# Last attention of a two-layer kernel: values weighed in two phases of two query tiles instead of three phases

## The chip, the cores and the metric

The kernel runs on one core of a Trainium2 chip. The metric is the device time of one execution in microseconds (us); the median of three runs is 1755.78 us (1751.4 to 1757.81).

## The reference

Four sequences of 512 tokens with 256 features pass through two layers. Each layer is an attention and a feed-forward part, each behind a layer norm and added to the residual stream:

1. a linear attention with decay in blocks, and a feed-forward part with Walsh-Hadamard transforms;
2. a softmax attention without a mask (16 heads of 16 features), and then a block that holds a causal attention and a mixture of experts.

The change lies in that last block. Its attention has 32 query heads of 64 features over 8 key and value heads and rotary tables; the mixture takes 4 of 16 experts for each token:

```python
q, k = _rope(q, k)                                   # 32 query heads, 8 key/value heads of 64
k = jnp.repeat(k, g, axis=2)
v = jnp.repeat(v, g, axis=2)
scores = jnp.einsum('bqhd,bkhd->bhqk', q, k) / np.float32(np.sqrt(HEAD_DIM))
scores = jnp.where(causal[None, None], scores, jnp.float32(-1e+30))
attn = jax.nn.softmax(scores, -1)
o = jnp.einsum('bhqk,bkhd->bqhd', attn, v).reshape(B, S, NHEADS * HEAD_DIM)
x = x + o @ wo
h = _rms(x, ff_ln_w)
logits = h @ wg
topv, topi = jax.lax.top_k(logits, TOP_K)
gate = jax.nn.softmax(topv, -1)
```

## The kernel before, in words

The stages follow one another: first layer, attention of 16 heads, last attention, mixture of experts. The order of the instructions in the last two is written out by hand, so each engine runs its queue in the order of the program text. The last attention takes from about 694 us to 1435 us of the span.

**Units and steps.** A unit `u` (16 of them) is one sequence and one pair of key/value heads: 8 query heads, four query tiles `t` of 128 tokens. A unit has five steps `f`, and the main loop counts them as `n = 5u + f`; `v = u - 1` is the unit before. In every step `fill(n)` puts scores into four PSUM banks (`sc`, one for each of four row groups `s`), `least(n)` on VectorE masks them into `masked` and takes the smallest of each row (the scores are negated), `exps(n, s)` on ScalarE makes exponentials in place and their sums, and one step later `turn_blocks(n)` on VectorE transposes blocks of 32 x 32 into `pT`. `FILLS` says which query tiles a step holds: before, tile 3 takes steps 0 and 1 (one half of the heads `jj` each), tiles 0 and 2 share steps 2 and 3, tile 1 has step 4. `masked` has one buffer for each `s`, so `least(n)` follows `turn_blocks(n - 1)`; the four `sc` banks have one set, so `fill(n + 1)` follows `least(n)`.

**Weighing the values.** `weigh(u, phase, ...)` multiplies `pT` by the values. It works on tiles of 32 rows by 64 columns of the array: for each chunk `c` of 32 keys, each row group `a` of four and each half `g`, one product whose moving operand is 4 heads x 32 queries = 128 columns, or 256 columns where two query tiles of a phase still need that chunk. A product stands as two matmul instructions in the profile (fp32). Its sums stay in four banks (`heaps`). Before there are three phases: `"3"` (tile 3 alone, 16 chunks, at the end of step 4), `"02"` (tiles 0 and 2, 12 chunks, end of step 0 of the next unit) and `"1"` (tile 1, 8 chunks, end of step 1). `weighed` on VectorE multiplies the heap by the widened inverse sums into `oT`, at the start of the next step, ahead of that step's `turn_blocks`.

**Inverse sums and output.** `invert` takes reciprocals, `widen` on ScalarE spreads them over 64 columns, `inverses` transposes them on TensorE and copies them to `rsb`; `out_proj` multiplies `oT` by the output weights, and ScalarE and GpSimd add the result to `zs`.

**Banks.** Eight PSUM banks: four for `sc`, and four (`unit`) that all else shares in turn: heaps, `pq` of the inverses, `py` of the output, `pr` of the rotary projections (`q_lo`, `q_hi`, `keys_lo`, `keys_hi`), `pv` of the values, and those of the routing. A heap of four banks thus waits until the last four users have been copied out. These copies are held back by `drain` and placed among the exponentials by the string of the step: a `.` is one held copy, a `w` one `widen`, a digit one `exps`. What is left over goes after the exponentials.

**Extra pieces.** Layer norms of the next sequence and the routing of the one before (`route(b)`, ending in `choose` and 16 scatters into `xs`) are queues of small pieces, of which `extras(plain, banked, scatters)` takes a few per step. `plan_tiles(0)` then makes the tables of the first expert tiles, and `read_plan(0)` reads them. `plan_tiles(1)` and the routing of the last sequence are pieces among the expert tiles.

**Transfers.** `spread(u, i)` loads a quarter of the values of unit `u` into `vsr` by four transfers on the SP queue; `fetch_q`, `twice` and the writes to `vd` use the same queue.

Of the kernel before, what the change touches and what calls it, by code (L numbers as in the profile page):

```python
# [16 lines left out]
P = 128  # L17
B = 4
S = 512
# [70 lines left out]
def kernel(  # L90
# [1207 lines left out]
    with ExitStack() as a2:  # L1298
# [20 lines left out]
        def spread(u, i):  # L1319

            if i == 0:
                vsrs[u] = ap2.tile([P, 16, P], F32, tag="vsr", bufs=2, name="vsr")
            part = slice(4 * i, 4 * i + 4)
            for a in range(4):
                nc.sync.dma_start(
                    out=vsrs[u][rows(a), part, :], in_=vds[u // 2][u % 2, :, part, :]
                )
# [3 lines left out]
            ((3, 0, 0),),  # L1331
            ((3, 1, 0),),
            ((0, 0, 0), (2, 0, P)),
            ((0, 1, 0), (2, 1, P)),
            ((1, 0, 0), (1, 1, 2 * P)),
        )

        PARTS = {"3": ((3, 0),), "02": ((0, 0), (2, P)), "1": ((1, 0),)}
        PHASE_OF = ("3", "3", "02", "02", "1")
# [47 lines left out]
        def turn_blocks(n):  # L1387

            u, f = divmod(n, 5)
            phase = PHASE_OF[f]  # L1390
            if (u, phase) not in turned:
                turned[u, phase] = [
                    ap2.tile([P, 4, S], F32, tag=f"pT{g}", bufs=2, name="pT4")
                    for g in range(2)
                ]
            for s, p in enumerate(probs.pop(n)):
                dst = turned[u, phase][s % 2]
                if f < 4:
                    nc.vector.transpose(dst[:, 2 * (f % 2) + s // 2, :], p)  # L1399
                else:  # L1400
                    for jj in range(2):
                        nc.vector.transpose(
                            dst[:, 2 * jj + s // 2, : 2 * P],
                            p[:, 2 * P * jj : 2 * P * (jj + 1)],
                        )


        def weigh(u, phase, lo, hi):
            if lo == 0:
                heaps[u, phase] = [  # L1410
                    unit("po4") for _ in range(4)
                ]
            for c in range(lo, hi):
                for a in range(4):
                    on = [
                        i for i, (t, _) in enumerate(PARTS[phase]) if 4 * t + a >= c
                    ]
                    if not on:
                        continue
                    first, last = on[0], on[-1] + 1  # L1420
                    for g in range(2):
                        src = turned[u, phase][g][rows(a), :, :]
                        if len(on) == 2:
                            src = src.rearrange("p j (x n) -> p x j n", n=P)
                            src = src[:, 0:2, :, 32 * c : 32 * c + 32]
                        else:
                            at = PARTS[phase][first][1] + 32 * c
                            src = src[:, :, at : at + 32]
                        nc.tensor.matmul(  # L1429
                            heaps[u, phase][a][  # L1430
                                64 * g : 64 * g + 64, first * P : last * P
                            ],
                            lhsT=vsrs[u][rows(a), c, 64 * g : 64 * g + 64],
                            rhs=src, start=(c == 0), stop=(4 * PARTS[phase][first][0] + a == c),
                            skip_group_check=True,
                        )

        def invert(n):

            u, f = divmod(n, 5)  # L1440
            if f in (1, 3, 4):
                for t, _ in PARTS[PHASE_OF[f]]:
                    nc.vector.reciprocal(lots[u, "rs"][:, t, :], lots[u, "sm"][:, t, :])
# [8 lines left out]
        def inverses(u, t):  # L1452

            pq = unit("pq4")
            wide = wides.pop((u, t)).rearrange("p (j g) n -> p j (g n)", g=2)
            for j in range(4):
                nc.tensor.transpose(pq[:, tok(j)], wide[:, j, :], ident)  # L1457
            rsb[u, t] = ap2.tile([P, S], F32, tag="rsb", bufs=2, name="rsb")
            to = rsb[u, t]
            drain(lambda: nc.scalar.copy(to, pq))  # L1460

        def weighed(u, phase):
            heap = heaps.pop((u, phase))
            del turned[u, phase]
            for i, (t, _) in enumerate(PARTS[phase]):
                inv = rsb.pop((u, t)).rearrange("p (j n) -> p j n", j=4)
                oTs[u, t] = ap2.tile([P, 4, P], F32, tag="oT4", bufs=3, name="oT4")
                for a in range(4):
                    nc.vector.tensor_tensor(  # L1469
                        oTs[u, t][:, :, 32 * a : 32 * a + 32],  # L1470
                        heap[a][:, i * P : (i + 1) * P].rearrange("p (j n) -> p j n", j=4),
                        inv[:, :, 32 * a : 32 * a + 32], ALU.mult,
                    )

        def out_proj(u, t):
            py = unit("py4")
            oT = oTs.pop((u, t))
            for j in range(4):
                nc.tensor.matmul(  # L1479
                    py[:, :D], lhsT=oT[:, j, :], rhs=wo4[:, 4 * (u % 4) + j, :],  # L1480
                    start=(j == 0), stop=(j == 3),
                )
            z = zs[u // 4][:, t, :]

            def leave():
                y = ap2.tile([P, D], F32, tag="y4", bufs=2, name="y4")
                nc.scalar.copy(y, py[:, :D])  # L1487
                nc.gpsimd.tensor_tensor(z, z, y, ALU.add)  # L1488

            drain(leave)  # L1490
# [225 lines left out]
        def plan_tiles(phase):  # L1716

            lo, hi = PHASES[phase]
            pos = C("iota")

# [8 lines left out]
            wide = [P, NEXP, NEXP]  # L1729
# [9 lines left out]
            nc.vector.tensor_tensor(tiles, tiles, taken, ALU.subtract)  # L1739
            nc.vector.tensor_tensor(  # L1740
# [3 lines left out]
            nc.vector.tensor_reduce(first, cube, AX.X, ALU.add)  # L1744
            mine, past = small("mine"), small("past")
# [6 lines left out]
            if phase == 0:  # L1752
# [20 lines left out]
                nc.vector.tensor_tensor(place, place, ahead, ALU.add)  # L1773
            info = rp.tile([P, 5, NEXP], F32, tag="info", name="info")
# [83 lines left out]
        for n in range(5 * NU + 4):  # L1858
# [12 lines left out]
            if u % 4 == 0 and f == 4 and 0 < u < 4 * B:  # L1871
                later.extend(route(u // 4 - 1))
                if u // 4 == B - 1:
                    later.append((False, lambda: plan_tiles(0)))
                    later.append(("pause", lambda: None))
                    later.append((False, lambda: read_plan(0)))
# [7 lines left out]
            if on and u % 2 == 0:  # L1884
                if u > 0 and f < 4:
                    spread(u, f)
                if f == 4:
                    spread(u + 1, 0)
            elif on and f < 3:
                spread(u, f + 1)  # L1890
# [4 lines left out]
            if f < 3 and v >= 0:  # L1895
                weighed(v, ("3", "02", "1")[f])
            if 0 < n <= 5 * NU:
                turn_blocks(n - 1)
                invert(n - 1)
            if v >= 0:  # L1900
                if f == 0:
                    inverses(v, 0)
                    inverses(v, 2)
                if f == 1:
                    inverses(v, 1)
                    out_proj(v, 3)
                if f == 2:
                    out_proj(v, 0)
                    out_proj(v, 2)
                if f == 3:  # L1910
                    out_proj(v, 1)
            if on:
# [6 lines left out]
                if f == 4:  # L1919
                    inverses(u, 3)  # L1920
                    q_hi(2 * u + 3)
# [5 lines left out]
                if f == 1 and u % 2 == 1:  # L1927
                    extras(0, 1)


                wide = {0: [(v, 1)] if v >= 0 else [], 3: [(u, 3)], 4: [(u, 0), (u, 2)]}
                for i in ("..w0123", "..0.1.23", ".0.12.3", "w.0.12.3", ".ww.0123")[f]:
                    if i == "w":
                        if wide[f]:
                            widen(*wide[f].pop(0))
                    elif i == ".":
                        drain_one()
                    else:
                        exps(n, int(i))
            elif f == 0 and v >= 0:  # L1940
                widen(v, 1)
# [7 lines left out]
            if f == 0 and v >= 0:  # L1949
                weigh(v, "02", 0, 12)  # L1950
            if f == 1 and v >= 0:
                weigh(v, "1", 0, 8)
                del vsrs[v]
            if f == 4 and on:
                weigh(u, "3", 0, 16)
# [9 lines left out]
        pieces += [lambda: plan_tiles(1)] + 5 * [lambda: None] + [lambda: read_plan(1)]  # L1965
# [332 lines left out]
```

## Time and profile before

| What | Value |
|---|---|
| median of three runs | 1755.78 us |
| profiled execution: time, span | 1759.42 us, 1757.6 us |
| TensorE clock granted, mean | 0.962 |
| TensorE busy | 1626.2 us (93%) |
| VectorE, ScalarE, GpSimd busy | 1011.9, 826.7, 895.9 us |
| matmul instructions of `weigh` (L1429) | 8064 |
| `fill` of unit 0 starts; weights of the first expert are issued | 693.8 us; 1435.5 us |
| a unit, mean over units 1 to 12 | 44.9 us |

In the profile a group of instructions stands as line, engine, operation, output<-inputs, shapes and count, then its busy time and the mean of one instruction, then the idle time of the engine before it with what ended that idle time. In a timeline the first two columns are start and length in us, and square brackets hold the idle time before. Lengths of matmuls are modelled: they overlap one another, so that a start is worth more than an end. L numbers are lines of the kernel.

### The profile page before, as it was taken

Reading aid. Unit: us, or ns where it says so; the run is one execution under the profiler, and the core shown is the slowest. Engines: PE = TensorE matmul, PEld = TensorE weight load, DVE = VectorE, ACT = ScalarE, POOL = GpSimd, SP = SyncE. Lnnn points to the kernel's source line nnn. Section 1 sums busy time; section 2 is a strip of 40 time slices with the busy share of each in tenths; the row PEclk is TensorE's granted clock in tenths of the full one; section 3 lists DMA queues with packets and bytes.
Section 4 is the critical chain, followed back from the end, with each engine's and each line's share of the span. In section 5 each row is a group of like instructions: output and inputs, shape, how many; then the busy total and the mean of one; then the engine's idle time right before and its main releaser. Section 6 shows DMA issues by size and latency. Waiting matters only on the chain.

```text
span 1757.6 us, 42136 instructions
## 1 busy us (share of the span) xinstructions
PE 1626.2 (93%) x16100; PEld 952.7 (54%) x16100; DVE 1011.9 (58%) x3097; ACT 826.7 (47%) x2170; POOL 895.9 (51%) x914
## 2 busy tenths in 40 slices
PE   7999999999999999899999999999999858899993
PEld 4665554553333334566666666666666635455551
DVE  4547336556665613767776686768766934433333
ACT  4431122126555575566666666665656514233331
POOL 4224133216555496655466647795577145744442
PEclk9999999999998899999999999999999969899997
DMA  9992000010000011222222222222132047655556
GB/s 358 370 371 87 0 1 0 1 55 1 1 1 1 1 31 48 92 56 56 54 59 56 56 56 56 84 75 59 43 86 70 3 164 225 147 87 87 87 87 167
DMA packets 106935, 146.60 MB, mean 83 GB/s; under 512 B 11632, under 2 KB 86128, under 8 KB 106352
## 3 DMA queue, kind: packets, MB, share of 16 engines
q1 hardware_dynamic: 91856, 123.54, 22.9%
q0 software_dynamic: 14448, 19.80, 6.5%
q8 instruction: 131, 2.15, 0.5%
q14 instruction: 68, 0.56, 0.1%
q10 hardware_dynamic: 432, 0.55, 0.1%
HBM read 67.17 MB, written 68.29 MB: 77 GB/s over the span
## 4 chain that ended last, share of the span: by engine, by line
PE 75%; DVE 7%; ACT 6%; POOL 5%; issue 4%; DMA 2%; SPq 0%; DVEq 0%; ACTq 0%; POOLq 0%
PE ph L1991 8%; PE po L1429 8%; PE sc L1352 7%; PE pgu L225 6%; PE py L1479 6%; PE py L234 6%; PE pr L225 5%; PE sT L1164 5%; PE sc L329 4%; PE pyx L1991 4%; PE oT L1177 3%; PE pq L225 2%; ACT masked L1382 2%; PE pv L234 2%; PE pq L1457 1%
## 5 line engine op out<-in xcount | busy, mean ns | idle before, releaser
L1382 ACT ACTIVATE masked<-masked,mx 128x256 f32<-128x256 f32 (+3 forms) x512 | 281.1, 553 | 13.6 <-DVE mx L1370 13.6
L1370 DVE CUSTOM_DVE_ANT_0 masked<-sc,cst 128x256 f32<-128x256 f32 (+3 forms) x512 | 213.9, 480 | 18.5 <-PE sc L1352 18.5
L1429 PE MATMUL po<-pT,vsr 32*64 32x128 f32 (+1 forms) x8064 | 186.6, 286 | 31.0 <-issue 16.0
L1399 DVE STREAM_TRANSPOSE pT<-masked 128x512 f32<-128x512 f32 x256 | 168.1, 690 | 57.3 <-ACT masked L1382 56.9
L335 DVE TENSOR_REDUCE top<-sc 128x1 f32<-128x512 f32 x256 | 158.7, 681 | 62.0 <-PE sc L329 62.0
L1429 PEld LDWEIGHTS po<-pT,vsr 32*64 32x64 f32 x8064 | 153.3, 131 | 75.1 <-issue 26.8
L2073 POOL DMA_INDIRECT acc<-yx,goes x79 | 123.3, 1561 | 138.3 <-ACT yx L2072 98.7
L1352 PE MATMUL sc<-kr,qr 32*128 32x128 f32 (+3 forms) x2048 | 180.8, 467 | 7.0 <-DVE mx L1370 4.4
L1991 PE MATMUL ph<-wall,hTx 128*128 x316 | 162.6, 638 | 10.5 <-DVE hTx L2029 10.1
L1170 ACT ACTIVATE pT<-sT 128x512 f32<-128x512 f32 x256 | 131.7, 602 | 59.2 <-PE sT L1164 59.2
L1488 POOL TENSOR_TENSOR z<-z,y 128x256 f32<-128x256 f32 x64 | 47.5, 743 | 182.5 <-ACT y L1487 182.4
L1469 DVE TENSOR_TENSOR oT<-po,rsb 128x128 f32<-128x128 f32 x256 | 61.5, 286 | 119.1 <-PE po L1429 112.3
L2053 DVE TENSOR_TENSOR ax<-ph,gx 128x256 f32<-128x256 f32 x79 | 33.5, 424 | 163.8 <-ACT gx L2051 163.7
L1352 PEld LDWEIGHTS sc<-kr,qr 32*128 32x128 f32 x2048 | 95.0, 194 | 58.7 <-issue 32.2
L1012 POOL TENSOR_TENSOR part<-raw,rtab 128x512 f32<-128x512 f32 x80 | 102.7, 1284 | 46.3 <-ACT raw L1003 42.9
L1479 PE MATMUL py<-wo,oT 128*128 128x256 f32 x512 | 123.6, 390 | 1.6 <-DVE oT L1469 1.6
L225 PE MATMUL pr<-hT,wq 128*128 128x512 f32 x256 | 122.8, 603 | 0.0
L1164 PE MATMUL sT<-qr,km 32*128 32x512 f32 x512 | 110.5, 650 | 6.4 <-DVE top L335 3.5
L225 PE MATMUL pgu<-xnT,wug 128*128 128x512 f32 x256 | 114.5, 598 | 1.5 <-DVE xnT L190 1.5
L1479 PEld LDWEIGHTS py<-wo,oT 128*128 128x128 f32 x512 | 94.9, 193 | 30.0 <-DVE pT L1399 7.6
L1006 POOL TENSOR_TENSOR qr<-raw,rtab 128x512 f32<-128x512 f32 x64 | 80.9, 1286 | 33.1 <-ACT raw L1003 33.1
L1382 ACT ACTIVATION_READ_ACCUMULATOR masked<-masked,mx 128x1 f32 x512 | 97.6, 191 | 0.0
(307 smaller groups left out, 2823.6 us busy)
## 6 DMA issues: line engine op xcount, KB each, us to landing
xs<-zero SPq DMA_DIRECT2D x16, 2304.0 KB
vsr<-vd SPq DMA_DIRECT2D x256, 64.0 KB
wall<-in_w_exp_dram SPq DMA_DIRECT2D x16, 768.0 KB
xin<-xs SPq DMA_DIRECT2D x79, 144.0 KB
wq<-in_w_q_dram SPq DMA_DIRECT2D x33, 256.0 KB
kr<-krq SPq DMA_DIRECT2D x32, 256.0 KB
acc<-zero SPq DMA_DIRECT2D x2, 2176.0 KB
vd<-vs SPq DMA_DIRECT2D x64, 64.0 KB
```

Source lines behind the costliest of these rows:

```text
L225: nc.tensor.matmul(dst, lhsT=w[:, c, cols], rhs=srcT[:, c, tok], start=(c == 0), stop=(c == n - 1),)
L234: nc.tensor.matmul(dst, lhsT=srcT[:, i, tok], rhs=w[:, c, cols], start=(i == 0), stop=(i == len(chunks) - 1),)
L335: nc.vector.tensor_reduce(top[:, at : at + 1], sc, AX.X, ALU.max)
L1164: nc.tensor.matmul(us[g], lhsT=km[rows(g), tok(c)], rhs=qr[rows(g), :], start=True, stop=True,)
L1170: nc.scalar.activation(pT[:, g, :], us[g], AF.Exp)
L1352: nc.tensor.matmul(scs[s][:, at : at + w], lhsT=qrs[2 * u + jj][rows(s), ab, tok(t)], rhs=krs[u][rows(s), ab, :w], start=(ab == 0), stop=( ...
L1370: nc.vector.tensor_tensor_reduce(masked[:, part], sc[:, part], C("cmask")[:, S - (t + 1) * P :], 1.0, 3e38, ALU.add, ALU.min, mx[:, t, i : ...
L1382: nc.scalar.activation(part, part, AF.Exp, bias=lots[u, "mx"][:, t, i : i + 1], scale=-1.0, accum_out=lots[u, "sm"][:, t, i : i + 1],)
L1399: nc.vector.transpose(dst[:, 2 * (f % 2) + s // 2, :], p)
L1429: nc.tensor.matmul(heaps[u, phase][a][64 * g : 64 * g + 64, first * P : last * P], lhsT=vsrs[u][rows(a), c, 64 * g : 64 * g + 64], rhs=src ...
L1479: nc.tensor.matmul(py[:, :D], lhsT=oT[:, j, :], rhs=wo4[:, 4 * (u % 4) + j, :], start=(j == 0), stop=(j == 3),)
L1991: ins = nc.tensor.matmul(out, lhsT=lhsT, rhs=wall[:, bass.ds(w_at[i] + at, n)], **kw)
```

## The change

- `FILLS` is reordered: tiles 0 and 2 in steps 0 and 1, tile 1 in step 2, tile 3 in steps 3 and 4.
- `weigh` has two phases `h`: tiles 0 and 1 (8 chunks) at the end of step 4, tiles 2 and 3 (16 chunks) at the end of the next step 0. The products become 168 for a unit instead of 252; those of 256 columns become 104 instead of 20, those of 128 columns 64 instead of 232.
- `pT` is kept by phase, with one buffer instead of two; `vsr` has one buffer instead of two; its loads go to steps 1 to 4.
- `weighed` writes its result over the inverse sums in `rsb`: 8 instructions of 256 columns instead of 16 of 128.
- Inverses, widenings and output projections move between steps: one output projection in each of steps 0 to 3; tile 3's inverse is taken, widened and transposed in step 0 of the next unit.
- `plan_tiles` is a generator in four pieces; in the last three units `extras(0, 1)` is also called in the middle of steps 0 and 4, ahead of the exponentials.

```diff
-vsrs[u] = ap2.tile([P, 16, P], F32, tag="vsr", bufs=2, name="vsr")
+vsrs[u] = ap2.tile([P, 16, P], F32, tag="vsr", bufs=1, name="vsr")
 FILLS = (
-    ((3, 0, 0),),
-    ((3, 1, 0),),
     ((0, 0, 0), (2, 0, P)),
     ((0, 1, 0), (2, 1, P)),
     ((1, 0, 0), (1, 1, 2 * P)),
+    ((3, 0, 0),),
+    ((3, 1, 0),),
 )
-PARTS = {"3": ((3, 0),), "02": ((0, 0), (2, P)), "1": ((1, 0),)}
+STEP = (P, 3 * P)
+WIDTH = (3 * P, 7 * P)
+LAST_OF = {1: (0, 2), 2: (1,), 4: (3,)}
...
+def weigh(u, h):
+    heaps[u, h] = [unit("po4") for _ in range(4)]
+    step = STEP[h]
+    for c in range(8 * h + 8):
         for a in range(4):
+            on = [t for t in (2 * h, 2 * h + 1) if 4 * t + a >= c]
...
+def weighed(u, h):
+    oT = rsb.pop((u, h)).rearrange("p t (j n) -> p (t j) n", j=4)
+    for a in range(4):
+        part = oT[:, :, 32 * a : 32 * a + 32]
+        nc.vector.tensor_tensor(
+            part, heap[a][:, : 2 * P].rearrange("p (j n) -> p j n", n=32),
+            part, ALU.mult,
+        )
...
 # main loop
-later.append((False, lambda: plan_tiles(0)))
+plan = plan_tiles(0)
+later.extend(4 * [(False, lambda: next(plan, None))])
...
+if on and u > 0 and f > 0:
+    spread(u, f - 1)
 if on:
     fill(n)
-if f < 3 and v >= 0:
-    weighed(v, ("3", "02", "1")[f])
+if f == 0 and v >= 0:
+    invert(n - 1)
+    widen(v, 3)
+    weighed(v, 0)
+if f == 1 and v >= 0:
+    weighed(v, 1)
 if 0 < n <= 5 * NU:
     turn_blocks(n - 1)
+    if f > 0:
+        invert(n - 1)
+if f == 0 and v >= 0:
+    inverses(v, 3)
+if f < 4 and v >= 0:
+    out_proj(v, f)
+if f == 3 and on:
+    inverses(u, 0)
+    inverses(u, 2)
+if f == 4 and on:
+    inverses(u, 1)
...
-if f == 1 and u % 2 == 1:
+if f == 1 and u % 2 == 1 or f in (0, 4) and u > 12:
     extras(0, 1)
-wide = {0: [(v, 1)] if v >= 0 else [], 3: [(u, 3)], 4: [(u, 0), (u, 2)]}
-for i in ("..w0123", "..0.1.23", ".0.12.3", "w.0.12.3", ".ww.0123")[f]:
+wide = {2: [(u, 0), (u, 2)], 3: [(u, 1)]}
+for i in ("..0123", ".0.12.3", "..ww.0123", "..w.0.1.23", "..0123")[f]:
...
-    weigh(v, "02", 0, 12)
-if f == 1 and v >= 0:
-    weigh(v, "1", 0, 8)
+    weigh(v, 1)
...
-    weigh(u, "3", 0, 16)
+    weigh(u, 0)
...
-pieces += [lambda: plan_tiles(1)] + 5 * [lambda: None] + [lambda: read_plan(1)]
+plan2 = plan_tiles(1)
+pieces += 4 * [lambda: next(plan2, None)] + 4 * [lambda: None]
+pieces += [lambda: read_plan(1)]
```

## Prediction

> **What bounds the kernel now.** I read the page, then each unit of the last attention as a stretch of its own, the groups with their forms kept apart, the timelines of TensorE, VectorE and ScalarE over unit 10, and the end of the stage. First a stretch that is one unit, and the stage's main groups:
>
> ```profile
> core 0: us, PE busy (x) PEld busy (x) DVE busy (x) ACT busy (x) POOL busy (x), PEclk, DMA share, GB/s
> 827.00:868.00 41.00, 39.85 (x704) 27.65 (x700) 29.42 (x105) 26.36 (x81) 18.87 (x17) 1.00 0.18 45
> 1136.00:1181.00 45.00, 41.49 (x716) 27.73 (x712) 30.07 (x109) 27.97 (x86) 42.36 (x61) 1.00 0.28 84
> ```
>
> Unit 3, nearly free of extra pieces, takes 41.9 us from fill to fill, unit 10 45.1; the mean of units 1 to 12 is 44.9. TensorE is filled in both, VectorE at two thirds. In unit 10 GpSimd is full too.
>
> ```profile
> L1429 PE MATMUL po<-pT,vsr 32*64 32x128 f32 x7424 | 173.7, 277 | 30.9 <-issue 16.0 <-ACT raw L1003 11.3 <-ACT hT L989 3.0
> L1429 PE MATMUL po<-pT,vsr 32*64 32x256 f32 x640 | 43.7, 389 | 0.1
> ...
> L1399 DVE STREAM_TRANSPOSE pT<-masked 128x512 f32<-128x512 f32 x245 | 160.9, 690 | 51.8 <-ACT masked L1382 51.4
> L1469 DVE TENSOR_TENSOR oT<-po,rsb 128x128 f32<-128x128 f32 x256 | 61.5, 286 | 119.1 <-PE po L1429 112.3 <-ACT masked L1382 5.1
> L1402 DVE STREAM_TRANSPOSE pT<-masked 128x256 f32<-128x256 f32 x128 | 43.5, 406 | 0.0
> ```
>
> VectorE's `weighed` (L1469) waits 112 us for TensorE, so TensorE ends last. Now its row of work in unit 10:
>
> ```profile
> 1138.50 4.50 PE L1429 MATMUL po<-pT,vsr 32*64 32x256 f32 x168
> 1142.93 2.00 PE L1352 MATMUL sc<-kr,qr 32*128 32x512 f32 x16
> ...
> 1173.07 0.46 PE L1429 MATMUL po<-pT,vsr 32*64 32x128 f32 x12
> 1175.51 2.70 PE L1429 MATMUL po<-pT,vsr 32*64 32x128 f32 x170 [1.97 <-ACT raw L1003]
> 1179.39 1.33 PE L1429 MATMUL po<-pT,vsr 32*64 32x128 f32 x50 [1.18 <-issue]
> ```
>
> Phase "02" runs unbroken. Phase "3" stops after 12 matmuls: its fourth bank still holds `q_hi`'s `pr`, and ScalarE's copy of it waits for GpSimd:
>
> ```profile
> 1174.86 0.60 ACT L1003 ACTIVATE raw<-pr 128x512 f32<-128x512 f32 x1 [1.78 <-POOL qr L1006]
> ```
>
> Last, the end of the stage, where `plan_tiles(0)` holds VectorE from 1407.8 to 1416.2 ahead of `weighed`, and the first expert waits for rows:
>
> ```profile
> 1410.69 0.87 PE L1429 MATMUL po<-pT,vsr 32*64 32x128 f32 x15 [0.59 <-issue]
> 1417.36 1.09 PE L1457 MATMUL pq<-ident,wide 128*128 128x128 f32 x4 [5.80 <-DVE oT L1469]
> ...
> 1440.45 0.66 PE L2027 MATMUL ptx<-ident,xin 128*128 128x128 f32 x2 [10.22 <-DMA xin<-xs]
> ```
>
> **A. The products.** The columns moved stay the same (272 times 128 a unit); the instructions fall from 504 to 336. By the starts inside unbroken runs: 8 chunks of 128 columns last 2.08 us from first to last start, 16 last 4.28, phase "02" 4.24. In "02" (the run at 1047.70) the first chunk of 256 columns takes 0.83, the next three 0.44 each, and a chunk of 128 columns 0.26, the last three of a run 0.22. So 128 columns are paced by instructions (16 by 16.7 ns = 0.267) and 256 by columns (a lone row group repeats 128 columns every 109 ns: 4 x 109 = 0.436). After: phase 0 is 0.83 + 3 x 0.44 + 0.27 + 3 x 0.22 = 3.1; phase 1 is 0.83 + 11 x 0.44 + 0.27 + 3 x 0.22 = 6.6. Before 2.08 + 4.24 + 4.28 = 10.6, after 9.7, and there is one run's start and tail less, 0.1: -1.0 us a unit, **-16** for 16. Ends: 14 chunks of 256 columns at 0.52 (two of 128) instead of 0.44 take it all back, 0; a first chunk at 0.44 instead of 0.83 in one phase gives 0.4 more, -22.
>
> The Trainium skill ("TensorE: Matmul & The Clock Gate", section "Wait — 56ns, not 53.3ns?") says that matmuls never start closer than about 25 ns. By that floor 168 fewer would be -4.2 us a unit, -67 in all. The 232 starts in 4.28 us here are 18 ns apart, so the row decides.
>
> **B. The wait for a bank in step 4.** Starts that come late inside step 4 sum to 1.14 us a unit (units 1 to 12). After, two widenings no longer stand ahead of `q_hi`'s copy, and step 3 is longer, so GpSimd has freed the buffer. The copy still lands 0.35 to 0.5 late (like the 0.36 wait of phase "1"): -0.7 x 14 = **-10**; ends 0 and -16.
>
> **C. Steps 1 to 3 without a phase.** TensorE's work there falls from 24.9 us to 21.5 (even unit), so I walk the loop `least`, exponentials, transposes from the end of phase 1 (t = 0). Step 1: `weighed` to 0.8, eight transposes to 3.5, `least` 2.8 to 6.3; ScalarE, exponentials 1.0 for each `s` with the copies `y` 0.4 and `raw` 0.6 among them, to 9.9; last transpose 10.7, reciprocals, `least` of step 2 to 13.75. TensorE is free at 13.05 (fill 2.0, output 1.9, projections 1.75 each), so fill 3 waits 0.7. Step 2: ScalarE copies, then two widenings (to 14.85), then 4.0 of exponentials to 18.85; transpose 19.65; `least` to 22.3. TensorE: fill to 15.5, output 17.4, two inverses 18.5, projections to 22.0; fill 4 waits 0.3. Step 4: fill 24.1, inverse 24.7, `q_hi` 26.5, phase 0 with its bank at 27.2, to 30.2. Step 0: fill 32.2, inverse 32.8 (its widening is done at 31.0), output 34.7, phase 1 to 41.5; the transposes that phase 1 needs end at 34.3, just ahead of it. Odd units give 41.0. TensorE's own sum is 40.8, so new waits are 0.5 a unit; extra pieces fall on a loop without the slack of before (VectorE waits for ScalarE 0.9 us in step 2 and 1.8 in step 3, mean of units 2 to 11): I take +0.7 x 14 = **+10**. Ends: 0, and +3.2 a unit if no extra piece hides (VectorE 32.2 against 30.3 in unit 3, ScalarE 27.9 against 26.6), +45.
>
> **D. Pieces in the middle of steps 0 and 4.** By the queue, three of these calls take a piece with a bank: `turned_both` (13,4), `logits` (14,0), `places` (15,0). Their copies are the third held ones, and the string has two dots, so they leave after the exponentials, and the heap's fourth bank waits: 3.2, 2.4 and 1.5 by the same walk, **+7**; ends 0 and +12.
>
> **E. The end of the stage.** `choose` comes four steps earlier; tables and scatters are done before step 4 of unit 15. Gone: the 5.8 above, and 4 us of scatters ahead of the last sum (1430.7 to 1434.8), which releases the first weights at 1435.5. Back: the 6.5 us of the first three table pieces (1407.8 to 1414.3) fall in step 1 of unit 15, where VectorE is last; 1.5 hide beside exponentials. The ranks in unit 14 add 1: +6. **-4**; ends -14 and +4.
>
> **F. Expert tiles.** Two tiles take 6.41 and 10.24 us against 3.25 around `plan_tiles(1)` (VectorE 1521.5 to 1526.8); the rest is SP's chain of transfers, which stays. In two iterations the lump hides in part: **-2**; ends -4 and +1.
>
> **At nothing.** `weighed`: 16 x 0.23 becomes 8 x 0.36 (between 0.34, the pace of 256-wide transposes, and 0.46), -0.8; eight more transposes +0.5; both lie beside TensorE, +0.3 a unit if not. `spread` waits on SP for phase 1 and holds `fetch_q`, `vd` and later loads behind it by up to a step; the last quarter is issued some 13 us before chunk 12 reads it, and a load of 82 KB was there 3 us after its issue (1418.5 to 1421.5). In the open it would be about 2 us a unit (four issues take 1.8 on SP). GpSimd and its projections keep their steps.
>
> **Sum:** -16 - 10 + 10 + 7 - 4 - 2 = -15. The span 1757.6 becomes 1742.6; the profiled execution takes 1.8 more (1759.42) and lies 3.6 above the median: **1741**.
>
> **The rivals.**
> - *Slower: the loop takes over.* `least`, exponentials and transposes end last in steps 1 to 3 and every extra piece adds. Then a unit is 41.3 + 1.8 (TensorE's extra work: 42.6 busy against 40.8 in unit 3) + 3.2 = 46.3, +17 over 12 units, with D +7, E and F -4: +20, 1776. It decides once steps 1 to 3 (22.3 us) exceed about 23.4. For: ScalarE has two copies and two widenings ahead of step 2's exponentials. Against: VectorE still idles some 2 us a step. The clock adds to it: six stretches of 3.4 us between 781 and 1400 are granted at half (0.57 over 781 to 785), 1.7 us each, and more waits may bring more of them.
> - *The loop hardly shows.* A and B as summed, C at +3, D absorbed, E -10, F -3: -36, 1720.
> - *It saves no time.* 256 columns at 0.52 a chunk: A 0 and the rest +1, 1757.
>
> The Trainium skill (same page, "What's actually happening") halves TensorE's clock after about 3.4 us of idleness. That speaks against steps with waits; by it one such stretch a unit would be an estimate of +1.7 x 16 = 27. In unit 10, with waits of 2.0 and 1.2 us, the row shows 1.00.
>
> **How the numbers follow.** Forecast 0.45 (1732 to 1752), loop unseen 0.22, no saving 0.10, slower 0.23. The range 1714 to 1778 takes in both outer cases and leaves their far ends out (0.06 below, 0.13 above). 0.5% is 8.8 us, about what a measurement of this kernel can tell from no change. Below 1747 lie 0.32 of the first and all of the second: 0.54; between 1747 and 1765 0.13 + 0.10: 0.23; above 0.23.
>
> **What would show it.** L1429 at 5376 instructions; phase 1 unbroken at 6.6 us, phase 0 at 3.1; unit 3 at about 41.3; waits of `sc` for `mx` in step 3 below 1 us; waits of phase 0 or 1 after 12 to 16 matmuls in (13,4), (14,0), (15,0); no 5.8 us gap at the end. I am wrong if phase 1 lasts over 7.5 us, if fills wait over 1.5 us for `mx` in steps 2 and 3, or if phase 1 waits for transposes.

## The result, and the profile after

The median goes from 1753.59 us (four runs, 1744.84 to 1757.81) to 1728.36 us (four runs, 1725.17 to 1740.61): 0.9856 of before, 95% interval 0.9819 to 0.9893. The forecast was 1741.0. The profiled execution of after took 1726.86 us, its span 1725.1 us at a mean clock of 0.963 (before 1757.6 at 0.962). The profiled executions thus differ by 32.6, the medians by 25.2; the parts below add up to the 32.6 but for rounding. The median lies below the 1732 to 1752 that the prediction gave to its forecast, on the side of "the loop hardly shows" (1720).

The stretches that are units 3 and 10 (columns as in the prediction's first view):

```profile
core 0: us, PE busy (x) PEld busy (x) DVE busy (x) ACT busy (x) POOL busy (x), PEclk, DMA share, GB/s
812.00:853.00 41.00, 40.86 (x559) 27.68 (x555) 30.61 (x109) 27.05 (x84) 21.18 (x20) 1.00 0.21 53
1108.00:1151.00 43.00, 40.72 (x548) 26.42 (x545) 30.66 (x109) 27.93 (x86) 40.52 (x59) 1.00 0.29 88
```

TensorE still fills a unit that is nearly free of extra pieces, with a fifth fewer instructions: unit 3 takes 40.4 us instead of 41.9, unit 10 43.1 instead of 45.1. The groups, forms apart:

```profile
L1428 PE MATMUL po<-pT,vsr 32*64 32x256 f32 x3328 | 143.6, 396 | 9.2 <-ACT h L989 2.9 <-ACT lg L1558 2.2 <-ACT raw L1003 2.0
...
L1428 PE MATMUL po<-pT,vsr 32*64 32x128 f32 x2048 | 90.6, 283 | 0.0
...
L1468 DVE TENSOR_TENSOR rsb<-po,rsb 128x256 f32<-128x256 f32 x128 | 44.6, 411 | 72.3 <-PE po L1428 68.6 <-ACT junk L1499 3.7
```

3328 + 2048 = 5376 instructions of `weigh` instead of 8064. The idle time ahead of the narrow ones, 30.9 us before, is 0.0; that ahead of the wide ones goes from 0.1 to 9.2. TensorE's row of work in unit 10:

```profile
1146.49 0.67 PE L1428 MATMUL po<-pT,vsr 32*64 32x256 f32 x12
1148.14 2.82 PE L1428 MATMUL po<-pT,vsr 32*64 32x256 f32 x92 [0.98 <-ACT raw L1003]
...
1155.15 6.80 PE L1428 MATMUL po<-pT,vsr 32*64 32x256 f32 x232
```

Phase 1 is one unbroken run, 6.53 or 6.54 us from first to last start in every one of units 2 to 12. Phase 0 (3.4) still stops after 12 matmuls, for the bank of `q_hi`, in unit 10 for the reason that the prediction read before the change, ScalarE's copy behind GpSimd:

```profile
1147.49 0.60 ACT L1003 ACTIVATE raw<-pr 128x512 f32<-128x512 f32 x1 [2.03 <-POOL qr L1006]
```

And the end of the stage, where the gap of 5.8 us for `plan_tiles(0)` is gone and the wait for the first rows is 6.38 instead of 10.22:

```profile
1395.91 6.86 PE L1428 MATMUL po<-pT,vsr 32*64 32x256 f32 x232
1402.70 5.45 PE L1477 MATMUL py<-wo,rsb 128*128 128x256 f32 x24
1414.53 0.66 PE L2022 MATMUL ptx<-ident,xin 128*128 128x128 f32 x2 [6.38 <-DMA xin<-xs]
```

Where the 32.6 us come from, by the starts of `fill`: units 1 to 12 -29.5, unit 0 -3.6, unit 13 -1.7, unit 14 **+11.5**, unit 15 to the first expert product -2.1, expert stage -6.6, and -0.5 ahead of unit 0.

### The profile page after: what moved, and what is told of

Read it like the earlier page. It is cut to its first block, busy times and chain, and to the rows that moved or that the text cites. A ratio compares the mean times of both kernels' runs of the same rounds, so it can differ in the third digit from the quotient of the medians.

```text
span 1725.1 us, 36698 instructions
## 1 busy us (share of the span) xinstructions
PE 1620.5 (94%) x13412; PEld 941.9 (55%) x13412; DVE 1028.1 (60%) x3097; ACT 825.9 (48%) x2170; POOL 897.1 (52%) x914
## 4 chain that ended last, share of the span: by engine, by line
PE 75%; DVE 10%; ACT 7%; issue 3%; POOL 2%; DMA 1%; SPq 0%; DVEq 0%; ACTq 0%; POOLq 0%
PE ph L1986 9%; PE po L1428 8%; PE pgu L225 7%; PE sc L1355 6%; PE pr L225 6%; PE py L234 6%; PE py L1477 5%; PE sT L1164 5%; PE sc L329 4%; PE pyx L1986 4%; PE oT L1177 3%; ACT masked L1385 3%; PE pv L234 2%; DVE masked L1373 2%; PE pq L225 2%
## 5 line engine op out<-in xcount | busy, mean ns | idle before, releaser
L1385 ACT ACTIVATE masked<-masked,mx 128x512 f32<-128x512 f32 (+3 forms) x512 | 281.0, 553 | 15.6 <-DVE mx L1373 15.5
L1405 DVE STREAM_TRANSPOSE pT<-masked 128x512 f32<-128x512 f32 (+3 forms) x512 | 229.9, 489 | 51.5 <-ACT masked L1385 47.5
L1373 DVE CUSTOM_DVE_ANT_0 masked<-sc,cst 128x512 f32<-128x512 f32 (+3 forms) x512 | 213.8, 480 | 2.8 <-PE sc L1355 2.8
L1355 PE MATMUL sc<-kr,qr 32*128 32x256 f32 (+3 forms) x2048 | 182.8, 457 | 10.1 <-DVE mx L1373 9.2
L1428 PE MATMUL po<-pT,vsr 32*64 32x256 f32 (+1 forms) x5376 | 171.6, 353 | 9.2 <-ACT h L989 2.9
L1428 PEld LDWEIGHTS po<-pT,vsr 32*64 32x64 f32 x5376 | 137.5, 135 | 52.2 <-issue 18.3
L1355 PEld LDWEIGHTS sc<-kr,qr 32*128 32x128 f32 x2048 | 98.8, 187 | 67.0 <-issue 26.3
L1477 PE MATMUL py<-wo,rsb 128*128 128x256 f32 x512 | 134.3, 409 | 0.0
L1477 PEld LDWEIGHTS py<-wo,rsb 128*128 128x128 f32 x512 | 97.3, 200 | 38.7 <-ACT masked L1385 9.9
L1485 ACT COPY y<-py 128x256 f32<-128x256 f32 x64 | 23.6, 369 | 171.3 <-PE py L1477 171.2
```

What stands on the lines that cost most here:

```text
L1355: nc.tensor.matmul(scs[s][:, at : at + w], lhsT=qrs[2 * u + jj][rows(s), ab, tok(t)], rhs=krs[u][rows(s), ab, :w], start=(ab == 0), stop=( ...
L1373: nc.vector.tensor_tensor_reduce(masked[:, part], sc[:, part], C("cmask")[:, S - (t + 1) * P :], 1.0, 3e38, ALU.add, ALU.min, mx[:, t, i : ...
L1385: nc.scalar.activation(part, part, AF.Exp, bias=lots[u, "mx"][:, t, i : i + 1], scale=-1.0, accum_out=lots[u, "sm"][:, t, i : i + 1],)
L1405: nc.vector.transpose(turned[u, h][s % 2][:, 2 * jj + s // 2, to : to + w], p[:, at : at + w],)
L1428: nc.tensor.matmul(heaps[u, h][a][64 * g : 64 * g + 64, first * P : 2 * P], lhsT=vsrs[u][rows(a), c, 64 * g : 64 * g + 64], rhs=src, start ...
L1477: nc.tensor.matmul(py[:, :D], lhsT=oT[:, t % 2 * 4 + j, :], rhs=wo4[:, 4 * (u % 4) + j, :], start=(j == 0), stop=(j == 3),)
```

## A cause that no term had priced: waits for instructions

The runs of `weigh` in units 1 to 12 last 154.0 us before and 119.7 after, counted from first to last start. Of the 34.3 us, 9.4 are a shorter wait at the 12th matmul (the bank: 13.7 before, 4.3 after, beyond the 0.18 and 0.23 us that this start takes without a wait). 15.1 more, beyond the usual spacing, are ten waits of 0.8 us or more that come late in a run, mostly in phase "3", and end with "issue": the engine waited for nothing that the profile names. They are not there after. This is one of them, in unit 14 of before:

```profile
1358.30 0.46 PE L1429 MATMUL po<-pT,vsr 32*64 32x128 f32 x12
1359.11 3.14 PE L1429 MATMUL po<-pT,vsr 32*64 32x128 f32 x199 [0.36 <-ACT raw L1003]
1363.23 0.89 PE L1429 MATMUL po<-pT,vsr 32*64 32x128 f32 x21 [0.98 <-issue]
```

And these are the transfers of before from 1358 to 1364 us, in slices of 0.15 us:

```profile
GB/s 0 0 0 0 0 0 0 0 0 0 0 0 0 0 0 0 0 55 0 109 0 0 0 0 0 0 0 0 0 0 0 0 0 0 0 0 0 0 0 0
...
q8 instruction: 1, 0.02, 1.1%
```

The 20th slice (1360.85 us) holds one packet of 16384 bytes on a queue of kind "instruction" (109 GB/s x 0.15 us); it lands at 1361.91, and the matmul that waited starts 1.32 us later. In the trace this is the rule. Counted are matmuls from 700 to 1440 us that start 0.8 us or more after the one before, with idle time that ends with "issue", and 1.0 to 1.7 us after the end of a packet on this queue; the sums are from start to start:

| Kernel | Waits | Sum, us |
|---|---|---|
| before | 15 | 22.4 |
| b_route, b_str (before's products) | 14, 13 | 20.7, 21.9 |
| b_wide (before's products, phase "3" at half the pace) | 0 | 0 |
| narrow, narrow2 (after's products split) | 17, 23 | 17.8, 37.0 |
| after, and after once more | 0, 0 | 0, 0 |
| dot3, held, best, best2, nomid2 | 0 | 0 |

That the queue carries TensorE's instructions, 256 to a packet, can be counted: the profile of before has 33515 instructions of TensorE (matmuls, weight loads and its sequencer's own) and 131 packets, and 131 times 256 is 33536. Numbered in the order of their starts, the matmuls that waited stand at fixed places: with n packets landed, all 82 of the table, in five kernels, have the number 256n + 193 or 256n + 194. So TensorE waited at the same place of a block each time, a whole number of blocks on, as an engine does that has used up all that had come. In before, b_route, narrow and narrow2 no idle time that ends with "issue" and so long a distance between two starts stands anywhere else in these 740 us.

The Trainium skill ("Runtime: NRT & Kernel Launch", section "Instruction fetch mechanics") says that an engine's instructions are loaded in blocks of 16 KiB, 256 instructions, while the ones before run, and that this is mostly hidden. The packets agree on the block; for these matmuls it is not hidden. Each comes with a weight load, so a block holds 128 pairs. The last 128 ahead of the waits in phase "3" of units 1, 2, 4, 6 and 8 start within 1.8 to 1.9 us, while in the thirteen profiles no two packets of this queue start less than 3.23 us apart (730 to 1400 us). After, 128 matmuls of 256 columns take 3.5 us, about as long as a block needs.

The whole profile counts them too, first before, then after (packets, MB, share):

```profile
q8 instruction: 131, 2.15, 0.5%
```

```profile
q8 instruction: 109, 1.79, 0.4%
```

Both waits with "issue" in the prediction's views were of this kind: the matmul at 1179.39 starts 1.37 us after a packet's end, the one at 1410.69 1.51 us after.

## The experiments

The eleven ran in three sets, each on a chip of its own with before beside it: narrow, dot3, held and b_route (before 1757.78 us); b_wide, b_str, narrow2 and best (before 1779.96); after_again, best2 and nomid2 (before 1776.94). So kernels are compared through before on their own chip. On the chips of the second and third set TensorE's products also stop for 0.4 to 0.7 us at a time in the later units, half of these stops or more while GpSimd's scatters run, in before's products as in after's; what does it was not tried.

### narrow: after's wide products split, neighbours on the same tile

```diff
-nc.tensor.matmul(heaps[u, h][a][64*g:64*g+64, first*P:2*P], ...)   # 256 columns
+for g in range(2):
+    for t in on:                                                   # 128 columns each
+        nc.tensor.matmul(heaps[u, h][a][64*g:64*g+64, x*P:x*P+P], ...)
```

The two query tiles of a bank begin their sums one after the other here, and part of the first is not kept.

> The changed kernel, with every product of 256 columns of weigh written as two of 128 (same columns, same phases, same order): 8064 matmul instructions again. Theory (256 columns are paced by columns, 128 by instructions at 16.7 ns): a chunk of two tiles takes 32 x 16.7 = 0.53 us instead of 0.44, phase 1 goes from 6.5 to about 7.4 us, phase 0 from 3.4 to about 3.7, unit 3 from 40.4 to about 41.6, the whole +15 to +20 us over the changed kernel (about 1745). Rival (the gain came from the order and the waits for banks alone): phases and time within 3 us of the changed kernel. A floor of 25 ns between starts would make it +67.

1785.07 us, 1.0171 of before (1.0117 to 1.0225): by the ratios some 55 us more than after, much above what was expected. Its matmul instructions are 8704, not 8064, since before had 20 products of 256 columns in each unit. Phase 1 at the start of unit 3:

```profile
825.12 6.97 PE L1423 MATMUL po<-pT,vsr 32*64 32x128 f32 x320
833.07 2.06 PE L1423 MATMUL po<-pT,vsr 32*64 32x128 f32 x80 [0.98 <-issue]
```

Phase 1 lasts 8.1 to 8.9 us without its waits of 0.6 us or more in units 1 to 11, some 21 ns an instruction, and there are waits besides, which at this point had no name. That products sent four in a row to one tile of the array are slower was one reading, the number of instructions another.

### narrow2: the same split, neighbours on different tiles

```diff
+for t in (2 * h, 2 * h + 1):
+    for a in range(4):
+        for g in range(2):
+            nc.tensor.matmul(heaps[u, h][a][64*g:64*g+64, x*P:x*P+P], ...)
```

> After, with every product of 256 columns split in two of 128 again, in an order that goes over the four row groups and both halves before it returns to the same tile of the array (narrow sent two or four in a row to the same tile). As there, the banks of two query tiles do not hold the reference's sums. Theory: 128 columns are paced at 16.7 to 18 ns an instruction if neighbours go to different tiles, so phase 1 (400 instructions) takes 6.7 to 7.2 us and phase 0 (144) 2.4 to 2.6, 0.4 us a unit less than after's 9.9 in the sum; but instructions are then used up as fast as in before, and 1 to 2 us of waiting for them come back in a unit: +10 to +25 us over after, near before's time less 10. Rival (the pace of 25 ns in narrow belongs to the number of instructions, not to their order): phase 1 about 10 us again, +50 to +60 us.

1809.81 us, 1.0166 of before (1.0100 to 1.0232): as slow as narrow, for the other reason. Phase 1 at the start of unit 2:

```profile
779.39 3.07 PE L1422 MATMUL po<-pT,vsr 32*64 32x128 f32 x172
783.91 2.18 PE L1422 MATMUL po<-pT,vsr 32*64 32x128 f32 x128 [1.45 <-issue]
787.37 2.24 PE L1422 MATMUL po<-pT,vsr 32*64 32x128 f32 x100 [1.28 <-issue]
```

The starts are 15 ns apart between the two waits, and a phase 1 without its waits lasts 6.6 to 6.8 us in units 0 to 5, so narrow's 21 ns were its order. But between the two waits lie 128 matmuls exactly, one block of instructions, and two waits of 1.5 to 1.8 us in most units take back all that the pace gives: phase 1 lasts 9.8 to 10.2 us in units 1 to 6. The theory had 1 to 2 us of waiting in a unit; it is 2.9 to 3.6 where there are two, so its range was too low and the rival's time was right, for a reason that was not the rival's.

### b_wide: before, phase "3" at half the pace

```diff
+if phase == "3":
+    src = src.unsqueeze(1).to_broadcast([32, 2, 4, 32])
-heaps[u, phase][a][64 * g : 64 * g + 64, first * P : last * P],
+heaps[u, phase][a][64 * g : 64 * g + 64, first * P : end * P],   # end = last + 1 in phase "3"
```

> Before, with the products of phase "3" made 256 columns wide: the same 128 columns twice, the second copy into an unused half of the bank; the number of instructions and all else stay. New theory: 16 waits in the traces of before (24 us in all, 11 of them late in phase "3", 1.2 to 2.0 us each) end 1.2 to 1.6 us after a packet of 16 KB on the queue of TensorE's instructions has landed, so they are waits for instructions, which a run of 232 products and 232 weight loads uses up faster than they come. At half the pace (13 chunks at 0.44 and the last three at 0.33, 0.22 and 0.11: 6.4 us instead of 4.28 unbroken) these waits vanish: phase "3" 6.5 to 6.9 us in all units against a mean of 5.7 before, so +13 to +19 us on the whole. Rival (the waits have to do with banks or with other engines, not with the pace): they stay, phase "3" takes 7.8 to 8.2 us on the mean, +35 to +40 us.

1811.36 us, 1.0175 of before (1.0107 to 1.0243), +31 us. Phase "3" in unit 6, where before waits 1.73 us:

```profile
1002.50 0.67 PE L1432 MATMUL po<-pT,vsr 32*64 32x256 f32 x12
1003.34 7.12 PE L1432 MATMUL po<-pT,vsr 32*64 32x256 f32 x220 [0.16 <-ACT raw L1003]
```

The same 232 instructions, and no late wait in the phase "3" of units 0 to 8, 10, 11 and 14: the wait goes with the pace. By size alone the rival was nearer: +31 us, and a phase "3" of 8.1 us on the mean. What decides is that its late waits are gone. The run without them lasts 7.57 us and not 6.5 to 6.9: the chunks in its middle take 0.43, as assumed, but the first takes 0.87 with the bank's wait, and the last three 0.60, 0.65 and 0.22 instead of 0.33, 0.22 and 0.11. The phases of units 9, 12, 13 and 15 have the stops of this chip besides.

### b_str: before, the copy of `q_hi` ahead of the widenings

```diff
-for i in ("..w0123", "..0.1.23", ".0.12.3", "w.0.12.3", ".ww.0123")[f]:
+for i in ("..w0123", "..0.1.23", ".0.12.3", "w.0.12.3", "..ww0123")[f]:
```

> Before, with both held copies of step 4 ahead of its two widenings (the string ..ww0123 in place of .ww.0123), so that the heap's fourth bank is copied out sooner. The prediction's term B (a wait for the bank of q_hi, which goes): phase "3" no longer stops after 12 products and lasts 4.3 us in most units, -10 to -20 us. New theory (the bank costs 0.4 us a unit and the rest is waiting for instructions): the wait after 12 products stays near 0.4 since the copy follows the projection in either place, the late waits of 1.2 to 2.0 us stay in 9 to 12 units, and the time is within 5 us of before.

1786.32 us, 1.0029 of before (0.9985 to 1.0072): no change. Phase "3" in unit 6:

```profile
998.40 0.46 PE L1429 MATMUL po<-pT,vsr 32*64 32x128 f32 x12
999.24 2.25 PE L1429 MATMUL po<-pT,vsr 32*64 32x128 f32 x137 [0.38 <-ACT raw L1003]
1003.07 1.82 PE L1429 MATMUL po<-pT,vsr 32*64 32x128 f32 x83 [1.57 <-issue]
```

The wait at the 12th matmul keeps its 0.38 us, for the copy follows the projection in either place, and late waits of 1.2 to 2.3 us stay in 11 units.

### b_route: before with the routing and table edits alone

```diff
+plan = plan_tiles(0)
+later.extend(4 * [(False, lambda: next(plan, None))])
...
+if f == 1 and u % 2 == 1 or f in (0, 4) and u > 12:
...
+pieces += 4 * [lambda: next(plan2, None)] + 4 * [lambda: None]
```

> The kernel before, with the edits of routing and tables alone (tables in four pieces in both places, pieces in the middle of steps 0 and 4 of the last three units). Theory (most of the gain comes from the weighing): the 5.8 us gap and the scatters at the end of the stage go, the expert tiles gain 4 to 6, the bank waits of the middle pieces cost 6, so -8 us against the kernel before (-3 to -13), with units 1 to 12 unchanged at 44.9. Rival (the gain comes from routing and tables): -18 us or more.

1760.08 us, 1.0017 of before (0.9994 to 1.0040). Theory had -8 us, and no gain is measured. The expert stage gains 3.1 us, and units 13 to 15 up to the first expert product lose 5.2 (173.75 instead of 168.59); units 1 to 12 take 4.0 less, some 3.4 of it for two stretches at half clock fewer. So routing and tables alone give nothing, and the gain of the change has to come from the weighing and what moved with it.

### dot3: the copies of the middle pieces ahead of the exponentials

```diff
+order = ("..0123", ".0.12.3", "..ww.0123", "..w.0.1.23", "..0123")[f]
+if f in (0, 4) and u > 12:
+    order = "." + order
```

> The changed kernel, with a third held copy ahead of the exponentials in steps 0 and 4 of units 13 to 15, so that the copy of a routing piece taken in the middle of the step frees its bank before the heap asks for it. Theory (the bank waits of 2.8, 2.1 and 0.8 us, and the half clock that follows them, are time on the path): step 4 of unit 13 goes from 13.0 to about 9.5, step 0 of units 14 and 15 from 16.7 and 17.8 to about 13 and 14.5, together -9 us (-6 to -11). Rival (VectorE ends last in units 14 and 15, and takes the time back in the next steps): within 3 us of the changed kernel.

1723.35 us, 0.9822 of before (0.9778 to 0.9866); the interval overlaps that of after, so the gain is read from the profiles, whose spans are 1717.1 and 1725.1. Units 13 to 15 up to the first expert product take 168.1 us instead of 176.2. Step (13,4) goes from 12.98 to 8.53 us and (14,0) from 16.71 to 12.53, as expected, but (15,0) only from 17.84 to 17.00. In (14,0) phase 1 stood for the copy of the logits in after:

```profile
1293.47 0.67 PE L1428 MATMUL po<-pT,vsr 32*64 32x256 f32 x12
1296.34 7.96 PE L1428 MATMUL po<-pT,vsr 32*64 32x256 f32 x220 [2.20 <-ACT lg L1558]
```

In dot3 it is one run:

```profile
1287.47 6.64 PE L1428 MATMUL po<-pT,vsr 32*64 32x256 f32 x232
```

### held: no plain piece in step 4 of units 7 and 11

```diff
-3 if u > 12 else 2 if f in (2, 3) else 1, 1 if f in (2, 3) else 0,
+(
+    3 if u > 12 else 0 if (u, f) in ((7, 4), (11, 4))
+    else 2 if f in (2, 3) or (u, f) in ((8, 0), (12, 0)) else 1
+),
+1 if f in (2, 3) else 0,
```

> The changed kernel, with no plain piece in step 4 of units 7 and 11 and two in step 0 of units 8 and 12: the routing piece of two VectorE operations (earlier) no longer stands between the last masks of a unit and the reciprocal of tile 3. Theory (that piece delays reciprocal, widening and the inverse that TensorE waits for in step 0): step 0 of units 8 and 12 goes from 15.3 to 11.0, -8 us in all. Rival (the delay only moves to step 1 of the same units): within 3 us of the changed kernel.

1725.96 us, 0.9817 of before (0.9775 to 0.9858): not told apart from after by its time, so the steps must say. Units 8 and 12 of after have a step 0 of 15.4 and 15.2 us, others 11.0. A routing piece stands ahead of tile 3's reciprocals on VectorE, so ScalarE widens late, and TensorE waits for it. VectorE in after:

```profile
1192.77 1.58 DVE L1585 TENSOR_TENSOR both<-both,cst 128x512 f32<-128x512 f32 x1
1194.38 1.64 DVE L1588 TENSOR_TENSOR both<-both 128x512 f32<-128x512 f32 x1
1195.94 0.19 DVE L1439 RECIPROCAL rs<-sm 128x8 f32<-128x8 f32 x1
```

TensorE in after:

```profile
1196.83 0.66 PE L1453 MATMUL pq<-ident,wide 128*128 128x128 f32 x4 [1.93 <-ACT wide L1444]
```

In held both steps take 11.8 us, but step 3 of both units takes 9.81 instead of 8.16, so the gain is some 3.6 of the 7 us, where 8 were expected. Each unit still has one stretch of 3.4 us at half clock: in after it begins in step 0 (1023.7 and 1197.8), in held at 1055.2 and 1225.8.

### best and best2: held and dot3 together, run twice, and after beside it

> After, with the edits of held (no plain piece in step 4 of units 7 and 11, two in the next step 0) and of dot3 (a third held copy ahead of the exponentials in steps 0 and 4 of the last three units) together. Theory: both gains add, 3.5 us in each of units 8 and 12 less up to 1.7 each for a stretch at half clock, and 8 us in units 13 to 15: 10 to 14 us less than after's 1728.4, so 1714 to 1719, and 0.976 to 0.979 of before. Rival: they share the same cover, or the stretch at half clock falls elsewhere: no better than dot3's 1723.

> The kernel of best again, on the same chip as after: theory 10 to 14 us less than after, 0.976 to 0.979 of before; rival (the gain of best against before came from the chip, where before was slow): no better than 0.982.

> After itself once more, beside best2 on the same chip. From the first measurement 0.986 of before, 0.982 to 0.990. Theory (units 1 to 12 lose 1.3 to 1.6 us each that TensorE waited for instructions, and half a microsecond each of banks and pace): no wait over 0.8 us inside phases 0 and 1 of units 1 to 12 ends 1.2 to 1.6 us after a packet of instructions has landed.

best: 1734.09 us, 0.9746 of before (0.9698 to 0.9795). best2, on the chip of the third set: 1727.24 us, 0.9736 (0.9704 to 0.9767). After beside it: 1747.88 us, 0.9852 (0.9819 to 0.9886). The two edits add, and to more than forecast: 20.6 us between the medians of one chip, with intervals that lie apart. Units 13 to 15 up to the first expert product take 179.5 us in best2 and 191.6 in after there; that after suffers more from that chip's stops is likely, but not shown. After beside it has no wait for instructions of 0.8 us or more, as its theory said.

### nomid2: held, and no pieces in the middle of steps

```diff
-if f == 1 and u % 2 == 1 or f in (0, 4) and u > 12:
+if f == 1 and u % 2 == 1:
```

> After with the edit of held, and without the pieces in the middle of steps 0 and 4 of the last three units. Theory: the three pieces with a bank must then go into steps 2 and 3, one each, so routing ends one and a half units later, after the last attention; phases 0 and 1 lose their waits (8 us), but the tables and scatters lie open behind unit 15: 0 to 15 us more than held's 1726, first expert product more than 15 us after the last product of phase 1. Rival (the queue has slack): as best, 10 us less than held.

1720.86 us, 0.9694 of before (0.9650 to 0.9738): 27 us less than after on that chip, the lowest of all ratios, though its interval overlaps best2's. The theory got the place right and the price wrong. The wait for the first rows is long, 14.32 us:

```profile
1391.13 5.45 PE L1477 MATMUL py<-wo,rsb 128*128 128x256 f32 x24
1410.90 0.66 PE L2026 MATMUL ptx<-ident,xin 128*128 128x128 f32 x2 [14.32 <-DMA xin<-xs]
```

But unit 14 takes 41.2 us instead of 54.7 in after on this chip (41.24 in the profile of before), and from the start of unit 13 to the first product of an expert's weights it is 175.4 us, against 191.6 in after and 179.5 in best2. So by these profiles the middle pieces cost more inside the stage than they give at its end, by 16 us against after, and by 4 against best2, which one profile of each does not settle.

## Why the prediction was right, and where it was wrong

The direction was right, and that the gain lies in the weighing. The time was 12.6 us too high, and the forecast came that near because errors in its terms have both signs. Two runs of before that step A rests on, phase "3" of unit 5 (two rows) and phase "1" of unit 6:

```profile
950.16 0.46 PE L1429 MATMUL po<-pT,vsr 32*64 32x128 f32 x12
950.98 3.73 PE L1429 MATMUL po<-pT,vsr 32*64 32x128 f32 x220 [0.36 <-ACT raw L1003]
1015.72 2.35 PE L1429 MATMUL po<-pT,vsr 32*64 32x128 f32 x104
```

Step by step, on the profiled spans:

- **A, direction right, half the size.** The "unbroken" 4.28 us of phase "3" was not unbroken: every phase "3" of before stops after 12 matmuls, the run of 4.28 in unit 5 too, while phase "1" of unit 6 does not stop. The same stop makes a phase "1" last 2.53 instead of 2.08 us, 0.45 more, so a free phase "3" is 3.84 and before's three phases 10.16. After's are 9.62 (3.09 without the wait in phase 0, and 6.53; forecast 3.1 and 6.6). Pace is thus worth 0.54 us a unit, 6.5 of the 34.3 us, where the forecast had 1.0 a unit. With 9.4 for the bank and 15.1 for late waits, 3.3 are left for shorter stops and slow starts. The floor of 25 ns that the prediction cites, which would have made it -67, does not hold for these matmuls: narrow2's start 15 ns apart on the mean, and the closest within a chunk 6 to 7 ns. And "paced by instructions" had a second meaning that the step missed: the same instructions must also be loaded.
- **B, another cause than was read.** The eight late waits of 0.8 us or more in phase "3" of units 1 to 12 sum to 13.7 us, which is the 1.14 a unit of "starts that come late inside step 4"; all eight are waits for instructions. The bank's wait in step 4 is 0.58 us a unit beside them and falls to 0.36. That the bank costs 9.4 us less in 12 units, 0.8 a unit where the forecast had 0.7, is luck: most of it (6.7 us) is the like wait of phase "1", which goes with that phase. The waits for instructions vanish whole: 15.1 us in the runs and some 3 in two fills (that end at 736.84 and 956.00), and no term had a price for them. The shown row with 1.18 "<-issue" was the sign, and no term asked what issue was.
- **C, too small, and in another place.** The walk's new waits in steps 1 to 3 hardly show: unit 2 takes 21.45 us in them, walked 22.3. Instead of a little in every unit, 8.6 us lie in step 0 of units 8 and 12, where the walk had said that the widening is done in time; it did not count the routing piece ahead of the reciprocals. Another 6 us are what is left in units 1 to 12: -29.5 against -34.3 - 3.0 (fills) - 6.8 (four stretches at half clock of before, 1.7 each) + 8.6. Together that is 14.6 where the forecast had 0.7 a unit, 8.4; what the 6 us are was not looked into.
- **D, near; E, wrong in sign.** Late starts in (13,4), (14,0) and (15,0) are 2.8, 2.1 and 0.8 us (3.2, 2.4 and 1.5). But units 13 to 15 up to the first expert product take 7.7 us more, with +11.5 in unit 14, where D + E were to add 3 and A to take 3 off. Neither counted the clock: from unit 13 to the end of unit 15's step 4 it is granted at half for 37.5 us, before for 6.8, by an estimate (half of the difference) worth up to 15 us where TensorE ends last. dot3 and nomid2 show that the middle pieces and their copies are behind most of the loss.
- **F, too small.** The expert stage gets 6.6 us shorter, not 2. The slots around `plan_tiles(1)` go from 6.41, 10.24, 3.72 and a plain 3.25 to 3.48, 3.75, 7.35 and 4.72, -4.3; the first slots give another 1.2. b_route has the like, 3.1 in all.
- **The rivals.** "The loop hardly shows" (1720) lies nearer than the forecast in time, but its D absorbed and E at -10 did not come. "It saves no time" falls with phase 1, whose chunks of 256 columns take 0.43 us and not 0.52. The slower one needed waits in steps 1 to 3, which are not there.

## What to carry to other kernels

When products are small and many, compare the time in which an engine uses up 256 instructions with the time between two packets of its instruction queue: here 128 matmuls within 1.8 us ran dry, and 128 within 3.5 us did not. A wait put down to "issue" late in a long run is a question to be answered before it is added to another term. Before filling a step with moved pieces, ask which short copy or reciprocal on the way to TensorE they will stand in front of.

## What the runs showed of the hardware that was not expected

- TensorE's instructions come in packets of 16384 bytes, 256 of them, never less than 3.23 us apart by their starts in thirteen profiles (730 to 1400 us), and a matmul that waited for one starts 1.2 to 1.6 us after the packet's end. Two such matmuls of narrow2 (783.91 and 787.37) lie 3.46 us apart: 128 starts at 15 ns and the wait of 1.55 us that follows them.
- Matmuls on 32 x 64 tiles with 128 columns start about 15 ns apart when neighbours go to different tiles (narrow2; a whole phase 1 without its waits 17 ns), and 21 ns apart in a whole phase 1 when up to four in a row go to the same one (narrow).
- A stretch of 3.4 us at half clock can follow a wait of about 2 us (from start to start): in after those of 2.4 us that end at 1022.90 and 1196.83 are followed by one at 1023.7 and 1197.8, in before three of 1.8 to 2.1 us by those at 781.2, 1091.8 and 1225.0. It is no rule: the wait of 2.2 us ahead of 1175.51 in before has none. The Trainium skill ("TensorE: Matmul & The Clock Gate", section "What's actually happening") puts it at some 3.4 us of idleness; here less was enough.
- The same VectorE operation of 512 columns (L1580 in after) took 0.68 us and 1.76 us; the three of 1.76 in the last attention start beside a running operation of GpSimd, the three of 0.68 while GpSimd is idle. It was not tried by itself.
